# Layer 0's weight folds as two fp32r products, with butterflies on GpSimd and input signs at the exit

## The chip, the cores and the metric

The kernel runs on one core of a Trainium2 chip. The metric is device time in microseconds (us) of one execution of the whole program; several runs are taken and their median is compared. The engines of the core are TensorE (PE in the profile; PEld are its weight loads), VectorE (DVE), ScalarE (ACT), GpSimd (POOL) and SyncE (SP), which here only issues transfers (DMAs). Each engine works through its own queue in order and waits there for what other engines deliver.

## The reference, cut to what matters

Two layers over x of shape 4 x 512 x 512. Each layer is a layer norm, a sequence block `s`, a feed-forward block whose silu is the gate `g`, and `x + s * g`. Layer 0's sequence block is softmax attention with 32 query and 8 key heads of 16. Its feed-forward block is the one that the change touches:

```python
x = fwht(x * SU_ug) / SCALE
x_up = x @ W_up.T * (Wscale_ug[:INTER] * SCALE)
x_gate = x @ W_gate.T * (Wscale_ug[INTER:] * SCALE)
x = silu(x_gate) * x_up
x = fwht(x * SU_dp) / SCALE
x = x @ W_down.T * (Wscale_dp * SCALE)
```

`fwht` is a Walsh-Hadamard transform over the last dimension (512, then 2048), with entries of +1 and -1 before its scale. `SU_ug` and `SU_dp` are vectors of signs. Layer 1 (a gated delta rule and a feed-forward block with signed weights) is not touched.

## The kernel before, in words

**Folding.** The transform is not applied to the activations but to the weights, once, in the first of the four batches: `W` becomes sign x Hadamard x `W`. A Hadamard matrix of 512 is a Kronecker product, so it is applied in two parts: butterflies (sums and differences) over the 4 chunks of 128 rows, and one product with a 128 x 128 Hadamard matrix over the rows of a chunk.

For gate and up weights there are 16 pairs `n` = 0 to 15, each 256 columns of one of the two matrices: a tile `raw` of 128 x 4 x 256 fp32. `load_raw(n)` (L166) loads it, `mix(n, 0)` and `mix(n, 1)` (L240) do the two butterfly levels, from `raw` to `tmp` and back, each level one sum and one difference of 128 x 512 elements (`butterfly`, L48, whose two operations are L52 and L53), on VectorE. `fold(n, j)` (L247), j = 0 and 1, multiplies two chunks by `hs`, the Hadamard matrix with the input signs in it, in fp32, into PSUM. From there ACT writes the product rounded to fp32r (a reduced fp32 that TensorE takes in one pass) as `hi` (L256), and VectorE the rest, `lo` = product - `hi` (L257). Both halves stand in the tile `fo`, which the gate/up products of batch 0 read and which a transfer stores (`wS`, L262) for the later batches. A plain fp32 product takes two passes on TensorE, so each shows as two matmul records.

For the down weights, `mix_down(q)` (L268), q = 0 to 15, multiplies a 128 x 512 piece by a 16-point Hadamard matrix `h16` held in 128 x 128, and writes it to DRAM in another order; `wdn` is loaded back from there (L275), and `fold_down(a)` (L279), a = 0 to 15, multiplies by `hmat` and scales (L282).

**Order.** The work runs in units `u` = 0 to 256. Unit `u` has one step of the attention of a batch (`maxima`: two score products L418 and a VectorE maximum over 1024 elements, L419; `exps`, 11 units later: two products L439 and an exponential on ACT, L441), and, from u = `LATE` = 16 on, one unit of feed-forward work: `v = u - 16`; in v = 0 to 31 of a batch one gate or up product of 8 matmuls (`gate_up`, L326, with its exits L332, L333, L336 on ACT and VectorE and the product L337 on GpSimd), in v = 32 to 63 the `down` products (L344). In batch 0 the folding is put in the units by the table `early`: `mix_down(q)` at u = q; pair `n`, with u = 12 + 2n as its base, has `mix(n, 0)` at base - 3, `mix(n, 1)` at base - 2, `fold(n, 0)` at base and `fold(n, 1)` at base + 1. `fold_down(a)` follows in v = 16 to 31. The library's scheduler may move an operation forward of this order when it holds it ready and the engine free; `keep_in_program_order` (here `inorder`) forbids that for single operations.

**Buffers.** `raw` has 3 buffers, `tmp` one, `fo` 3. The load of pair n + 3 is issued in `fold(n, 1)`. All pool `a0`, where these tiles lie, is given back at v = 32.

**GpSimd** has in this stage only L337 and, once in eight units, the attention's scaling L465. [...]

Of the kernel before, what the change touches and what calls it, by code (L numbers as in the profile page):

```python
# [18 lines left out]
P = 128  # L19
# [3 lines left out]
KC = DM // P  # L23
# [10 lines left out]
def kernel(ctx: ExitStack, tc: tile.TileContext, i: dict, out: bass.AP):  # L34
# [66 lines left out]
    if True:  # L101
# [64 lines left out]
        def load_raw(n):  # L166
            q, m = n // 2, n % 2
            raws[n] = new(a0, [P, KC, CQ], F32, "raw", bufs=3)
            nc.sync.dma_start(
                raws[n], i[("w_gateT", "w_upT")[m]][:, ts(q, CQ)].rearrange("(k p) n -> p k n", p=P)  # L170
            )
# [13 lines left out]
        for q in range(NI):  # L185
            if q in (0, 6, 12):
                load_raw(q // 6)
            nc.sync.dma_start(stage[q], i["w_downT"].rearrange("(p q) n -> q p n", q=NI)[q])
# [20 lines left out]
        for h in (8, 16, 32, 64, 1, 2, 4):  # L209
            nxt = new(a0 if h == 64 else awp, [P, P], F32, "h16" if h == 64 else "hmat", bufs=1 if h == 64 else 2)  # L210
            butterfly(nc.vector, nxt.unsqueeze(2), hmat.unsqueeze(2), P, h, inorder)
            hmat = nxt
            if h == 64:
                h16 = nxt
# [25 lines left out]
        def mix(n, stage):  # L240
            if stage == 0:
                tmps[n] = new(a0, [P, KC, CQ], F32, "tmp")
                butterfly(nc.vector, tmps[n], raws[n], KC, 1)
            else:
                butterfly(nc.vector, raws[n], tmps[n], KC, 2)

        def fold(n, j):  # L247
            q, m = n // 2, n % 2
            if j == 0:
                fos[n] = new(a0, [P, 2, 2, KC, P], F32R, "fo", bufs=3)  # L250
            ph = new(bmm, [P, 2, CQ], F32, "mm")
            for k in range(2):
                nc.tensor.matmul(ph[:, k, :], hs[:, 2 * j + k, :], raws[n][:, 2 * j + k, :], start=True, stop=True)
            ph = ph.rearrange("p k (c n) -> p c k n", n=P)
            hi, lo = fos[n][:, :, 0, 2 * j : 2 * j + 2, :], fos[n][:, :, 1, 2 * j : 2 * j + 2, :]
            nc.scalar.copy(hi, ph)  # L256
            nc.vector.tensor_tensor(lo, ph, hi, ALU.subtract)  # L257
            if j == 0:
                return
            if n + 3 < FF // P:  # L260
                load_raw(n + 3)
            nc.sync.dma_start(  # L262
                wS[ts(q, 2), m].rearrange("c p h k n -> p c (h k n)"),
                fos[n].bitcast(F32).rearrange("p c h k n -> p c (h k n)"),
            )


        def mix_down(q):  # L268
            ph = new(bmm, [P, DM], F32, "mm")
            nc.tensor.matmul(ph, h16, stage[q], start=True, stop=True)  # L270
# [8 lines left out]
        def fold_down(a):  # L279
            ph = misc()  # L280
            nc.tensor.matmul(ph, hmat, wdn[:, a, :], start=True, stop=True)
# [231 lines left out]
        ph = new(bmm, [P, KC, P], F32, "mm")  # L513
        for k in range(KC):
            hk = new(a0, [P, P], F32, "hk", bufs=1)
            inorder(nc.vector.tensor_scalar(hk, hmat, su_ug[:, k : k + 1], None, ALU.mult))
            nc.tensor.transpose(ph[:, k, :], hk, identf)
        hs = new(a0, [P, KC, P], F32, "hs")
        nc.scalar.copy(hs, ph)

# [3 lines left out]
        for n in range(FF // P):  # L524
            u = LATE + 2 * n - 4
            for d, f in ((-3, lambda n=n: mix(n, 0)), (-2, lambda n=n: mix(n, 1)),
                         (0, lambda n=n: fold(n, 0)), (1, lambda n=n: fold(n, 1))):
# [4 lines left out]
        for u in range(NU + LAG + 1):  # L532
# [22 lines left out]
            if 16 <= v < 16 + NI:  # L555
                fold_down(v - 16)
# [901 lines left out]
```

## Time and profile before

| | |
|---|---|
| median of 3 runs | 1493.79 us |
| lowest and highest run | 1490.02, 1494.76 us |
| span of the profiled execution | 1492.3 us |
| instructions in it | 22700 |
| TensorE, VectorE, ACT, GpSimd busy, whole span | 1429.4, 1035.8, 709.6, 313.5 us |
| first fold product L253, last one | 33.1, 164.7 us |
| `mix_down` products L270 | 19.1 to 41.5 us |
| gate/up products of batch 0 (L326 on `fo`) | 43.1 to 180.1 us |
| last butterfly half ends | 152.2 us |
| first `down` product L344 | 183.7 us |

The profile shows one execution. Its lines name an instruction by line of the kernel, engine, operation, tile written and tiles read. Groups give the count, the busy time in us and the mean of one in ns, then how long the engine stood idle before them and what ended that. A timeline line gives start, duration (us), engine, line, operation, and, in brackets, the idle time before it. Matmuls are pipelined: the duration of one record is longer than its distance to the next.

### The profile page before, as it was taken

The page shows a single profiled execution, that of the slowest core. Times are in us where ns is not written, and L with a number is a line of the kernel's source. Part 1 is how long each engine was busy: PE and PEld are TensorE (multiplying, and loading weights), DVE is VectorE, ACT ScalarE, POOL GpSimd, SP SyncE. Part 2 cuts the span into 40 slices and gives each one's busy share as a digit, 9 for nine tenths or more (in the row PEclk, how much of TensorE's full clock was granted, in tenths as well). Part 3 has the DMA queues.
Part 4 walks back from the last instruction along what each step waited for, and adds up shares of the span by engine and source line. Part 5 has one row for each costly group of instructions (what it writes and reads, how often), then busy time and mean ns, then how long its engine had stood idle before and what let it go on. Part 6 is the DMA issues. An engine that isn't in the chain of part 4 may idle for free. (4 is left out here: it accounts for less than half of the span.)

```text
span 1492.3 us, 22700 instructions
## 1 busy us (share of the span) xinstructions
PE 1429.4 (96%) x8144; PEld 855.6 (57%) x8144; DVE 1035.8 (69%) x1863; ACT 709.6 (48%) x1046; POOL 313.5 (21%) x304
## 2 busy tenths in 40 slices
PE   7999999999999999999999899999999999999998
PEld 3565533555335553356434576787568766776675
DVE  7999755765557655666525869768975799477746
ACT  4655554666446664466552434434353344323433
POOL 1112100322003220033100330045112531052001
PEclk9999999999999999999999999999999999999989
DMA  8865410475105741166103553434453354425532
GB/s 307 322 220 194 149 29 16 149 237 190 27 21 190 231 149 28 36 212 225 56 20 103 160 146 101 116 92 147 134 151 103 91 161 135 126 73 150 162 83 96
DMA packets 201793, 199.11 MB, mean 133 GB/s; under 512 B 65520, under 2 KB 153040, under 8 KB 200784
## 3 DMA queue, kind: packets, MB, share of 16 engines
q1 hardware_dynamic: 198624, 196.29, 41.9%
q10 hardware_dynamic: 3056, 1.37, 0.4%
q8 instruction: 64, 1.05, 0.3%
q14 instruction: 49, 0.40, 0.1%
HBM read 146.80 MB, written 46.19 MB: 129 GB/s over the span
## 5 line engine op out<-in xcount | busy, mean ns | idle before, releaser
L419 DVE TENSOR_REDUCE nmx<-sc 128x2 f32<-128x1024 f32 x256 | 312.3, 1220 | 159.1 <-PE st L439 147.3
L441 ACT ACTIVATE pe<-st 128x1024 f16<-128x1024 f32 x256 | 262.6, 1026 | 143.4 <-PE st L439 141.6
L344 PE MATMUL y<-wdn,hT 128*128 128x512 f32 x512 | 253.3, 617 | 3.0 <-DVE g L348 1.7
L326 PE MATMUL mm<-xr,wc 128*128 128x512 f32 x768 | 206.8, 410 | 0.0
L326 PEld LDWEIGHTS mm<-xr,wc 128*128 128x128 f32 x768 | 137.4, 189 | 48.4 <-issue 21.8
L337 POOL TENSOR_TENSOR hT<-hT,th 128x512 f32<-128x512 f32 x64 | 84.2, 1316 | 319.2 <-ACT hT L336 309.0
L344 PEld LDWEIGHTS y<-wdn,hT 128*128 128x128 f32 x512 | 87.0, 189 | 96.0 <-issue 88.5
L711 PE MATMUL pu<-xn1T,wp 128*128 128x512 f32 x288 | 129.9, 594 | 0.0
L941 PE MATMUL ph<-xsh,sg 128*128 128x512 f32 x256 | 113.0, 441 | 5.6 <-ACT sg L926 5.3
L418 PE MATMUL sc<-kT,qT 32*128 32x512 f16 x512 | 102.5, 385 | 7.8 <-DVE nmx L419 7.4
L926 ACT ACTIVATE sg<-sw 128x512 fp32r<-128x512 f32 x128 | 79.5, 625 | 55.2 <-PE y L972 32.2
L941 PE MATMUL ph<-xsl,sg 128*128 128x512 f32 x256 | 104.1, 407 | 0.7 <-DVE xsl L901 0.7
L418 PEld LDWEIGHTS <-qT 32*128 32x128 f16 x512 | 26.2, 91 | 131.8 <-issue 127.9
L465 POOL TENSOR_TENSOR oT<-os,sm 128x512 f16<-128x512 f32 x32 | 41.5, 1298 | 285.9 <-DMA sm<-rec_d 248.8
L439 PE MATMUL st<-qm,kT 32*128 32x512 f16 x512 | 100.0, 384 | 0.3 <-ACT pe L441 0.3
L946 ACT ACTIVATE hT<-ph,upsc 128x512 f32<-128x512 f32 x64 | 43.8, 685 | 94.3 <-PE ph L941 94.1
L711 PEld LDWEIGHTS pu<-xn1T,wp 128*128 128x128 f32 x288 | 54.0, 191 | 56.6 <-issue 54.8
L972 PE MATMUL y<-sg,hsh 128*128 128x512 f32 x256 | 83.0, 432 | 0.7 <-ACT sg L926 0.7
L1019 POOL TENSOR_TENSOR gm<-g,le 128x384 fp32r<-128x384 f32 x64 | 57.8, 921 | 83.0 <-PE pu L1020 52.0
L326 PE MATMUL mm<-xr,fo 128*128 128x512 f32 x256 | 73.2, 420 | 0.9 <-DVE fo L257 0.9
L972 PE MATMUL y<-sg,hsl 128*128 128x512 f32 x256 | 73.5, 400 | 0.0
L332 ACT ACTIVATE th<-mm,hwg 128x512 f32<-128x512 f32 x64 | 44.0, 688 | 56.0 <-PE mm L326 56.0
(302 smaller groups left out, 2370.2 us busy)
## 6 DMA issues: line engine op xcount, KB each, us to landing
wc<-wS SPq DMA_DIRECT2D x96, 512.0 KB
wS<-fo SPq DMA_DIRECT2D x16, 1024.0 KB
sw<-in_upT SPq DMA_DIRECT2D x64, 256.0 KB
sw<-in_downT SPq DMA_DIRECT2D x64, 256.0 KB
sm<-rec_d SPq DMA_DIRECT2D x128, 64.0 KB
raw<-in_w_gateT SPq DMA_DIRECT2D x8, 512.0 KB
hT<-in_w_downT SPq DMA_DIRECT2D x16, 256.0 KB
raw<-in_w_upT SPq DMA_DIRECT2D x8, 512.0 KB
```

The source lines that it names most:

```text
L326: nc.tensor.matmul(pgs[m], wcs[b, c, m][:, h, k, :], xrs[b][:, k, :], start=(k + h == 0), stop=(k == KC - 1 and h == 1))
L337: nc.gpsimd.tensor_tensor(hT, hT, ths[b, c], ALU.mult)
L344: nc.tensor.matmul(ys[t], hTs[b, c][:, ts(t, P)], wdn[:, c, :], start=(c == 0), stop=(c == NI - 1))
L418: nc.tensor.matmul(sc[:, j, :], qTs[n][rows, ts(t, P)], kTs[b, g // 4][rows, :], start=True, stop=True)
L419: nc.vector.tensor_reduce(nmxs[n][:, t, 2 * pr : 2 * pr + 2], sc, AX.X, ALU.max, negate=True)
L439: nc.tensor.matmul(st[:, j, :], kTs[b, g // 4][rows, ts(k, P)], qms[n][rows, :], start=True, stop=True)
L441: nc.scalar.activation(pes[u], st, AF.Exp)
L711: nc.tensor.matmul(pp, wps[b, n][:, k, 0:P], xn1Ts[b][:, k, :], start=(k == 0), stop=(k == KC - 1))
L926: tc.keep_in_program_order(nc.scalar.activation(sgs[b, c, m], raws[b, c, m], AF.Sign))
L941: ins = nc.tensor.matmul(ph, sgs[b, c, 0][:, ts(k, P)], xss[b][n][:, k, :], start=(k + n == 0), stop=(k == KC - 1 and n == 1))
L972: ins = nc.tensor.matmul(yss[b][t], hss[b, c][n][:, ts(t, P)], sgs[b, c, 1], start=(c + n == 0), stop=(c == NI - 1 and n == 1))
L1019: nc.gpsimd.tensor_tensor(gm, bc_in(s["g2"][:, t, u, x], P), bc_mid(le, 3), ALU.mult)
```

## The change

The products with the Hadamard matrix, whose entries are +1 and -1 and exact in fp32r, become two fp32r products: the other operand is split in a rounded half `hi` and a rest `lo`, by a new helper:

```diff
+        def halves_of(src, eng):
+            rh = new(a0, [P, 2, DM], F32R, "rh", bufs=2)
+            hi = rh[:, 0]
+            nc.scalar.copy(hi, src)
+            eng.tensor_tensor(rh[:, 1], src, hi, ALU.subtract)
+            return rh
+
+        rhs = {}
+
+        def part_raw(n, j):
+            rhs[n, j] = halves_of(raws[n][:, 2 * j : 2 * j + 2, :].rearrange("p k n -> p (k n)"), nc.vector)
+            if j == 1 and n + 2 < FF // P:
+                load_raw(n + 2)
```

The signs can't stand in the matrix any more when it is to be the same for all chunks; they are applied when the product leaves PSUM, chunk by chunk:

```diff
             for k in range(2):
-                nc.tensor.matmul(ph[:, k, :], hs[:, 2 * j + k, :], raws[n][:, 2 * j + k, :], start=True, stop=True)
-            ph = ph.rearrange("p k (c n) -> p c k n", n=P)
-            hi, lo = fos[n][:, :, 0, 2 * j : 2 * j + 2, :], fos[n][:, :, 1, 2 * j : 2 * j + 2, :]
-            nc.scalar.copy(hi, ph)
-            nc.vector.tensor_tensor(lo, ph, hi, ALU.subtract)
+                for h in range(2):
+                    nc.tensor.matmul(ph[:, k, :], hmr, rhs[n, j][:, h, ts(k, CQ)], start=(h == 0), stop=(h == 1))
+            for k in range(2):
+                kk = 2 * j + k
+                src = ph[:, k, :].rearrange("p (c n) -> p c n", n=P)
+                hi = fos[n][:, :, 0, kk, :]
+                nc.scalar.activation(hi, src, AF.Copy, scale=su_ug[:, kk : kk + 1])
+                nc.vector.scalar_tensor_tensor(
+                    fos[n][:, :, 1, kk, :], src, su_ug[:, kk : kk + 1], hi, ALU.mult, ALU.subtract
+                )
             if j == 0:
                 return
-            if n + 3 < FF // P:
-                load_raw(n + 3)
```

The butterflies go to GpSimd, the down products are split too (with the rest on GpSimd), and the loads, the matrices and the order follow:

```diff
-            raws[n] = new(a0, [P, KC, CQ], F32, "raw", bufs=3)
+            raws[n] = new(a0, [P, KC, CQ], F32, "raw", bufs=2)
...
-            if q in (0, 6, 12):
-                load_raw(q // 6)
+            if q in (0, 8):
+                load_raw(q // 8)
...
             if h == 64:
-                h16 = nxt
+                h16r = new(a0, [P, P], F32R, "h16r")
+                inorder(nc.vector.tensor_copy(h16r, nxt))
+        hmr = new(a0, [P, P], F32R, "hmr")
+        inorder(nc.vector.tensor_copy(hmr, hmat))
...
-                butterfly(nc.vector, tmps[n], raws[n], KC, 1)
+                butterfly(nc.gpsimd, tmps[n], raws[n], KC, 1)
             else:
-                butterfly(nc.vector, raws[n], tmps[n], KC, 2)
+                butterfly(nc.gpsimd, raws[n], tmps[n], KC, 2)
...
         def mix_down(q):
+            rh = halves_of(stage[q], nc.gpsimd)
             ph = new(bmm, [P, DM], F32, "mm")
-            nc.tensor.matmul(ph, h16, stage[q], start=True, stop=True)
+            for h in range(2):
+                nc.tensor.matmul(ph, h16r, rh[:, h], start=(h == 0), stop=(h == 1))
...
         def fold_down(a):
+            rh = halves_of(wdn[:, a, :], nc.gpsimd)
             ph = misc()
-            nc.tensor.matmul(ph, hmat, wdn[:, a, :], start=True, stop=True)
+            for h in range(2):
+                nc.tensor.matmul(ph, hmr, rh[:, h], start=(h == 0), stop=(h == 1))
...
-        ph = new(bmm, [P, KC, P], F32, "mm")
-        for k in range(KC):
-            hk = new(a0, [P, P], F32, "hk", bufs=1)
-            inorder(nc.vector.tensor_scalar(hk, hmat, su_ug[:, k : k + 1], None, ALU.mult))
-            nc.tensor.transpose(ph[:, k, :], hk, identf)
-        hs = new(a0, [P, KC, P], F32, "hs")
-        nc.scalar.copy(hs, ph)
...
             for d, f in ((-3, lambda n=n: mix(n, 0)), (-2, lambda n=n: mix(n, 1)),
+                         (-1, lambda n=n: part_raw(n, 0)), (0, lambda n=n: part_raw(n, 1)),
                          (0, lambda n=n: fold(n, 0)), (1, lambda n=n: fold(n, 1))):
...
-            if 16 <= v < 16 + NI:
-                fold_down(v - 16)
+            for a in range(NI):
+                if v == 8 + 3 * a // 2:
+                    fold_down(a)
```

So a pair's raw halves are split at base - 1 and base, `fold_down` stands in v = 8 to 30 instead of 16 to 31, and the tile `rh` with its two buffers is shared by the raw halves, `mix_down` and `fold_down`.

More of the change, by code (lines that the diff above doesn't have):

```diff
@@ L209 @@
         for h in (8, 16, 32, 64, 1, 2, 4):
[L210 removed]
+            nxt = new(a0, [P, P], F32, "hmat", bufs=2)
             butterfly(nc.vector, nxt.unsqueeze(2), hmat.unsqueeze(2), P, h, inorder)
```

## The prediction

> **What bounds the kernel now.** I read the slices first, then the stage in which the edited lines run, then its rows. The chain of waits covers only the kernel's last 110 us, so it says nothing of this stage.
>
> ```profile
> span 1492.3 us, 22700 instructions
> ...
> PE   7999999999999999999999899999999999999998
> ...
> DVE  7999755765557655666525869768975799477746
> ...
> POOL 1112100322003220033100330045112531052001
> ```
>
> A slice is 37.3 us. Over the whole span TensorE (PE) is the full row. VectorE (DVE) is full only in slices 2 to 4, and GpSimd (POOL) is nearly empty there. Those slices are layer 0's first batch, where the weights are folded. By stage (us; busy time of PE, weight loads, DVE, ACT, POOL; clock, DMA share, GB/s):
>
> ```profile
> 15.00:183.00 168.00, 159.94 (x759) 92.48 (x757) 153.95 (x224) 93.33 (x133) 27.59 (x20) 1.00 0.64 233
> ...
> 115.00:150.00 35.00, 32.00 (x150) 19.34 (x148) 34.97 (x48) 17.64 (x24) 8.71 (x6) 1.00 0.53 191
> 150.00:183.00 33.00, 32.37 (x160) 19.29 (x160) 25.60 (x42) 18.58 (x25) 6.38 (x5) 1.00 0.33 121
> ```
>
> From 115 to 150 us DVE is busy 34.97 of 35.00: it sets the pace, with PE close behind. After 150 us, when the butterflies are over, PE does. How far PE is from its own limit is seen in a later batch, whose gate/up units have no folds:
>
> ```profile
> 690.06 2.13 PE L326 MATMUL mm<-xr,wc 128*128 128x512 f32 x8
> ...
> 692.44 2.13 PE L326 MATMUL mm<-xr,wc 128*128 128x512 f32 x8
> ```
>
> 2.38 us a unit there. The first batch's 32 units run from 43.1 to 180.1 us, 4.28 us each. Everything after 183 us is untouched by the edit, so the change is worth what it moves the end of this stage.
>
> **DVE, part by part.** The rows of this stage (count | busy us, mean ns | idle before):
>
> ```profile
> L257 DVE TENSOR_TENSOR fo<-mm,fo 128x512 fp32r<-128x512 f32 x32 | 21.8, 681 | 2.9 <-ACT fo L256 2.9
> L53 DVE TENSOR_TENSOR tmp<-raw 128x512 f32<-128x512 f32 x16 | 14.1, 881 | 0.0
> L53 DVE TENSOR_TENSOR raw<-tmp 128x512 f32<-128x512 f32 x16 | 12.9, 808 | 0.0
> L52 DVE TENSOR_TENSOR raw<-tmp 128x512 f32<-128x512 f32 x16 | 11.9, 743 | 0.1
> ...
> L52 DVE TENSOR_TENSOR tmp<-raw 128x512 f32<-128x512 f32 x16 | 11.6, 728 | 2.5 <-DMA raw<-in_w_upT 1.3 <-DMA hT<-in_w_downT 1.1
> ```
>
> Off DVE go 64 butterfly halves (14.1+12.9+11.9+11.6 = 50.5 us), four `hk` scalings (4 x 0.28 = 1.1) and 32 old residues (21.8). On it come 32 residues of the raw weights (0.68 each by the butterflies' median: 21.8), and 64 residues of 256 elements from PSUM: 0.678 us at 512 elements (L333) and 0.352 at 192 (L1201) are 1.02 ns an element, so 0.42 each, 26.9. Two casts of the Hadamard matrix add 0.4. Net: -50.5 - 1.1 - 21.8 + 21.8 + 26.9 + 0.4 = **-24.3 us** before waiting.
>
> Waiting is the open price, because the new residues read two SBUF operands while GpSimd reads SBUF:
>
> ```profile
> 115.10 1.55 POOL L465 TENSOR_TENSOR oT<-os,sm 128x512 f16<-128x512 f32 x1 [1.28 <-DMA sm<-rec_d]
> ...
> 115.43 1.76 DVE L53 TENSOR_TENSOR raw<-tmp 128x512 f32<-128x512 f32 x1
> ...
> 144.54 1.28 POOL L465 TENSOR_TENSOR oT<-os,sm 128x512 f16<-128x512 f32 x1 [4.91 <-DMA wS<-fo]
> 144.56 0.67 DVE L257 TENSOR_TENSOR fo<-mm,fo 128x512 fp32r<-128x512 f32 x1
> ```
>
> The first pair reads SBUF on both sides: DVE took 1.76 us for what takes 0.68. In the second DVE reads one operand from PSUM, and nothing is lost. The butterflies lost on average (50.5 - 64 x 0.68)/64 = 0.11 us with POOL busy 27.6 of 168 us; the worst lost 1.1. With POOL nearly always busy, half of its 1.28 us is the middle: I take 0.6, bounds 0.11 and 1.1, so 32 x 0.6 = 19 us (3.5 to 35). DVE's net is then -5 us (-21 to +11).
>
> [...]
>
> **POOL.** On it come 64 butterfly halves, 16 residues in `mix_down` and 16 in `fold_down`; 16 products L337 and 4 of L465 are there already. Price of one, back to back:
>
> ```profile
> 641.19 1.29 POOL L337 TENSOR_TENSOR hT<-hT,th 128x512 f32<-128x512 f32 x1 [1.57 <-ACT hT L336]
> 642.44 1.17 POOL L485 TENSOR_TENSOR x<-sg,xin 128x512 f32<-128x512 f32 x1
> ```
>
> 1.25 us. Program order puts ahead of the last butterfly (unit 40) the 16 `mix_down` residues, 64 halves, 12 L337, 3 L465 and 11 `fold_down` residues: 106 x 1.25 = 132.5 us, from 15.4 us, when the first raw weights are there. [...] That is 15.4 + 132.5 + 19 = 167 us; the last butterfly ends at 152.2 today.
>
> **The raw buffers**, 3 to 2, and the load behind the raw residue instead of behind the fold. A load lands late:
>
> ```profile
> 102.97 0.37 SPq L169 DMA_DIRECT2D raw<-in_w_upT  x1
> ...
> 108.37 0.69 DVE L52 TENSOR_TENSOR tmp<-raw 128x512 f32<-128x512 f32 x1 [0.37 <-DMA raw<-in_w_upT]
> ```
>
> 5.4 us from issue to use. After a pair's second butterfly come two ACT copies and two DVE residues, behind a maximum of 1.22 us in DVE's queue (about 3.5 us), then 5.4 for the load: 8.9. POOL meanwhile has 4 halves (5.0), one L337 (1.25), 0.3 of L465, 1.2 of port and from unit 24 on 1.67 of `fold_down`: 7.8, later 9.4. So it idles about 1 us in the early pairs and little later; SP's queue adds to it, since L169 stands there behind stores that wait up to 5.8 us (L262). I take 0.7 us in 12 pairs: 8.5 us (0 to 18). Queued behind POOL's waiting butterfly are L337 and the `fold_down` residues; PE's folds wait for both.
>
> **The end by POOL.** 167 + 8.5 = 175.5. Then the last pair's copy, residue and fold, 0.62 + 1.28 + 0.78 + 0.37 + 0.42 = 3.5, and 1.0 of hand-overs: 180. Then the three units that need it or stand behind it, at 2.38 + 0.53 for a `fold_down`: 8.7, and 1.5 to the first `down`: **190.2 against 183.7**, +6.5.
>
> **PE.** `mix_down` and `fold_down`: six passes of L270 take 2.84 us, so (2.84 - 0.59)/5 = 0.45 a pass, two passes a product; fp32r of that shape takes 2.13/8 = 0.266. 32 x 2 x 0.18 = 11.5 us less. The folds keep their count: four fp32 passes of 256 take 0.78 (130.21 to 130.99); four fp32r lie between four weight loads, 0.75, and 4 x 0.266 = 1.06. I take 0.78, the same load count (-1 to +9 us in all). PE waits for POOL here, so this gain is in slack, as are the four transposes removed. **ACT** gains the 64 copies of high halves, 32 of raw weights and 32 for the two down steps (0.62 each, as L926 from SBUF: 39.7), and 64 scaled copies of 256 elements (0.37 each, between L256's 0.587 at 512 and L441's 1.025 at 1024, by the same slope: 23.7) in place of 32 of 0.587 (18.8); the `hs` copy, 0.6, goes. 93.3 + 44 = 137 of 168 us. Covered, unless it waits for `rh`, below. DMA bytes are unchanged; the second raw load goes out two `w_downT` loads later, covered by POOL's first 14 operations; moving `fold_down` to units 24 to 46 needs `wdn` earlier (84 instead of 115 us), and its loads go out at 51 today; some 15 us later still does.
>
> **Sum.** 1492.3 + 6.5, and the 1.5 us by which the median of the runs (1493.79) stands above the profiled span: **1500 us**.
>
> **The rivals.** *The relief wins.* For it: DVE is full and loses 24 us before waits; POOL's sum without port and idle loss is 15.4 + 132.5 = 148, earlier than today's 152.2. Then PE paces: 43.1 + 32 x 2.38 + 28 folds x 0.78 + 16 x 0.53 + 7 for values and queries = 156.7, 27 us earlier. Against: no engine stays idle long enough for all of that; half is -13: 1481. *The split buffers jam ACT*, the case on the slow side beyond mine: `rh` has two buffers for three users, one held by the raw half that waits for its fold. ACT's copy for `fold_down` or a raw half stands in order ahead of the exponentials; if it waits until POOL has passed one or two butterflies (1.25 to 2.5 us), 16 `fold_down` and 16 `mix_down` steps cost 32 x 1.9 = 61 us, of which ACT's slack 168 - 137 = 31 covers half. It decides once that wait exceeds 1 us a step: about +25 with part of the above, 1519. *Nothing moves*: DVE's 5 us net and POOL's 6 offset each other, 1494.
>
> **Chances.** POOL as bound, 1497 to 1510: 0.40. Relief: 0.29. Jam: 0.17. Nothing: 0.14. A measurement of this kernel tells 0.3% (4.5 us) from no change. Of my case 0.03 falls within it; of the nothing case 0.12, the rest on the sides: faster 0.30, same 0.15, slower 0.55. The range, 1479 to 1522, takes the relief down to its middle and the jam up to its own.
>
> **What would show it.** POOL busy over 85% from 20 to 165 us; residues of the raw weights above 1.1 us mean; the last butterfly after 165 us; the first `down` matmul near 190. The last butterfly before 150, or residues near 0.75, would show the relief; ACT copies waiting long for a PE release, the jam. I am wrong if POOL is not the last to deliver to the folds.

## The result, and the profile after

The changed kernel takes 1557.38 us (median of 4 runs, 1555.01 to 1558.02) against 1493.53 us: a ratio of 1.0431, 95% interval 1.0414 to 1.0448. The profiled execution has a span of 1555.5 us, 63.2 more than before. The forecast, 1500 us, had the direction, but the loss was ten times the size, and the range (to 1522) did not hold it.

The slices of the kernel after, to be read against those of before (a slice is now 38.9 us):

```profile
span 1555.5 us, 22937 instructions
...
PE   4787889999999999999999989999999999999998
...
DVE  5676775567655765566651687957994789567746
...
POOL 5457872022300322013310042025310541143001
PEclk9588879999999999999999999999999999999989
```

The first six slices, up to about 233 us, look different: before, PE was full from the second slice on and VectorE in three of them; now nothing is. PE stands at 4 to 8, VectorE at 5 to 7, and GpSimd, which my forecast had as the bound, at 4 to 8 as well. The granted clock, 1.00 in the stage before, is 0.5 in one of them. The windows of the kernel after show it by stage (busy time of PE, weight loads, VectorE, ACT, GpSimd; clock, DMA share, GB/s):

```profile
15.00:33.00 18.00, 11.55 (x61) 5.70 (x61) 9.49 (x19) 7.60 (x14) 10.99 (x9) 0.97 0.62 206
33.00:80.00 47.00, 34.62 (x94) 14.33 (x94) 26.90 (x36) 27.92 (x48) 23.68 (x19) 0.50 0.36 132
80.00:115.00 35.00, 28.57 (x142) 18.09 (x140) 28.07 (x45) 24.18 (x39) 18.74 (x15) 0.81 0.72 264
115.00:150.00 35.00, 25.82 (x116) 17.20 (x115) 19.66 (x29) 17.97 (x33) 25.61 (x20) 0.87 0.50 177
150.00:183.00 33.00, 28.28 (x109) 17.64 (x108) 24.45 (x34) 20.01 (x35) 26.31 (x20) 0.83 0.33 116
```

When every engine has gaps, the likely bound is a chain of hand-overs and not work. The waits of the kernel after between 15 and 240 us name its links (engine, tile and line that waited, who released it: us in total, times, longest):

```profile
POOL rh L254 <- ACT rh L253: 29.1, 14, 5.8
...
POOL hT L361 <- ACT hT L360: 23.2, 9, 5.0
ACT hT L293 <- PE mm L292: 22.7, 15, 4.6
DVE nmx L443 <- PE sc L442: 21.4, 13, 4.9
...
PEld mm L292 <- POOL rh L254: 13.7, 13, 4.6
ACT rh L253 <- POOL raw L52: 11.6, 8, 3.2
PEld y L305 <- POOL rh L254: 11.1, 8, 2.8
```

It is a ring: GpSimd's rest (L254) waits for ACT's high half (L253), PE's product (L292, L305) for GpSimd's rest, ACT's exit (L293) for PE's product, and ACT's next high half stands behind that exit. The timeline of the kernel after shows one turn in the `mix_down` stage (start, duration, engine, line; in brackets the idle time before):

```profile
34.56 1.14 ACT L253 CAST rh<-hT 128x512 fp32r<-128x512 f32 x2
...
35.24 2.14 PE L292 MATMUL mm<-rh,h16r 128*128 128x512 f32 x3 [0.65 <-ACT rh L253]
35.26 2.50 POOL L254 TENSOR_TENSOR rh<-hT,rh 128x512 fp32r<-128x512 f32 x2 [2.06 <-ACT rh L253]
...
37.41 0.59 ACT L293 COPY hT<-mm 128x512 f32<-128x512 f32 x1 [1.71 <-PE mm L292]
...
37.81 0.79 PE L292 MATMUL mm<-rh,h16r 128*128 128x512 f32 x1 [0.43 <-POOL rh L254]
...
38.64 0.59 ACT L293 COPY hT<-mm 128x512 f32<-128x512 f32 x1 [0.64 <-PE mm L292]
39.12 1.14 ACT L253 CAST rh<-hT 128x512 fp32r<-128x512 f32 x2
39.19 1.23 DVE L443 TENSOR_REDUCE nmx<-sc 128x2 f32<-128x1024 f32 x1 [3.33 <-PE sc L442]
```

Two steps take 4.56 us (34.56 to 39.12; the next turn begins at 43.70): 0.70 us to the first copy's hand-over, 1.25 for each of two rests, 0.79 for the last pass, an exit. The exit waits for the same last pass that sets a buffer of `rh` free, so this turn alone does not say whether the next copy waits for its place behind the exit or for the buffer. The maximum of the attention (L443) waits too, because its scores stand behind L292 in PE's order. In the timeline of the kernel before, the same product needed nothing but its loaded operand, and six passes, three steps, ran in 2.84 us:

```profile
26.91 2.84 PE L270 MATMUL mm<-hT,h 128*128 128x512 f32 x6
```

With the attention's work between them, the 16 steps took 22.4 us before and take 54.6 after.

In time: the first fold product comes at 54.6 us (33.1 before), the last at 231.4 (164.7), the first `down` at 246.0 (183.7). So of the 62.3 us by which this stage ends later, 21.5 are a later start of the folds, 45.2 a slower pace over the 16 pairs (176.8 us from first to last against 131.6), and 4.4 are regained behind the last fold. The rest of the kernel is as long as it was (1309.5 against 1308.6 us).

### The profile page after: what moved, and what is told of

Its sections match the earlier page's. It is cut to its first block, busy times and chain, and to the rows that moved or that the text cites. A ratio compares the mean times of both kernels' runs of the same rounds, so it can differ in the third digit from the quotient of the medians.

```text
span 1555.5 us, 22937 instructions
## 1 busy us (share of the span) xinstructions
PE 1447.3 (93%) x8140; PEld 865.8 (56%) x8140; DVE 1038.0 (67%) x1861; ACT 752.1 (48%) x1142; POOL 439.2 (28%) x400
## 5 line engine op out<-in xcount | busy, mean ns | idle before, releaser
L443 DVE TENSOR_REDUCE nmx<-sc 128x2 f32<-128x1024 f32 x256 | 312.4, 1220 | 183.0 <-PE st L463 149.8
L350 PEld LDWEIGHTS mm<-xr,wc 128*128 128x128 f32 x768 | 136.7, 188 | 48.2 <-issue 21.5
L442 PE MATMUL sc<-kT,qT 32*128 32x512 f16 x512 | 108.6, 400 | 12.5 <-DVE nmx L443 12.2
L463 PE MATMUL st<-qm,kT 32*128 32x512 f16 x512 | 106.2, 395 | 2.1 <-ACT pe L465 2.0
L944 ACT ACTIVATE sg<-sw 128x512 fp32r<-128x512 f32 x128 | 79.6, 625 | 57.2 <-PE y L990 33.1
L729 PEld LDWEIGHTS pu<-xn1T,wp 128*128 128x128 f32 x288 | 53.9, 191 | 56.6 <-issue 55.1
L350 PE MATMUL mm<-xr,fo 128*128 128x512 f32 x256 | 78.5, 449 | 2.2 <-ACT hT L360 1.4
```

The lines of the kernel that those rows point to most:

```text
L350: nc.tensor.matmul(pgs[m], wcs[b, c, m][:, h, k, :], xrs[b][:, k, :], start=(k + h == 0), stop=(k == KC - 1 and h == 1))
L442: nc.tensor.matmul(sc[:, j, :], qTs[n][rows, ts(t, P)], kTs[b, g // 4][rows, :], start=True, stop=True)
L443: nc.vector.tensor_reduce(nmxs[n][:, t, 2 * pr : 2 * pr + 2], sc, AX.X, ALU.max, negate=True)
L463: nc.tensor.matmul(st[:, j, :], kTs[b, g // 4][rows, ts(k, P)], qms[n][rows, :], start=True, stop=True)
L729: nc.tensor.matmul(pp, wps[b, n][:, k, 0:P], xn1Ts[b][:, k, :], start=(k == 0), stop=(k == KC - 1))
L944: tc.keep_in_program_order(nc.scalar.activation(sgs[b, c, m], raws[b, c, m], AF.Sign))
```

## The experiments

"Over before" is the ratio less one, times 1493.5 us. The three times on the right are those of the profiled execution: first and last fold product, first `down` product.

| kernel | ratio, 95% interval | over before, us | folds, us | `down`, us |
|---|---|---|---|---|
| before | 1 | 0 | 33.1 to 164.7 | 183.7 |
| after | 1.0431, 1.0414 to 1.0448 | 64 | 54.6 to 231.4 | 246.0 |
| e1_butterflies_only | 1.0043, 1.0025 to 1.0060 | 6 | 35.1 to 167.6 | 186.3 |
| e2_split_only | 1.0354, 1.0336 to 1.0372 | 53 | 43.5 to 223.8 | 239.0 |
| e3_mix_down_fp32 | 1.0271, 1.0249 to 1.0293 | 40 | 40.3 to 205.7 | 220.3 |
| e4_downs_fp32 | 1.0153, 1.0132 to 1.0174 | 23 | 38.1 to 190.2 | 206.1 |
| e9_downs_fp32_three_raw | 1.0078, 1.0051 to 1.0104 | 12 | 37.8 to 176.9 | 192.8 |
| e13_butterflies_signs | 1.0034, 1.0014 to 1.0055 | 5 | 34.4 to 169.0 | 187.6 |
| e5_three_rh | 1.0377, 1.0346 to 1.0408 | 56 | 48.6 to 218.3 | 232.9 |
| e6_own_rh | 1.0433, 1.0398 to 1.0468 | 65 | 69.5 to 229.7 | 244.8 |
| e7_kept_warm | 1.0427, 1.0399 to 1.0454 | 64 | 52.1 to 228.2 | 242.7 |
| e8_rest_on_dve | 1.0325, 1.0294 to 1.0355 | 49 | 46.8 to 207.6 | 223.5 |
| e16_after_the_norm | 1.0428, 1.0394 to 1.0462 | 64 | 52.4 to 231.8 | 246.4 |
| e19_half_ahead | 1.0358, 1.0324 to 1.0392 | 53 | 47.1 to 216.8 | 231.2 |
| e15_no_product_on_gpsimd | 1.0388, 1.0357 to 1.0418 | 58 | 53.9 to 225.2 | 240.5 |
| e18_mix_down_split | 1.0073, 1.0052 to 1.0093 | 11 | 43.2 to 177.2 | 196.0 |
| e12_fold_down_split | 0.9988, 0.9971 to 1.0006 | -2 | 35.1 to 164.9 | 182.3 |
| e17_fold_down_split_butterflies | 0.9979, 0.9960 to 0.9999 | -3 | 36.3 to 164.1 | 181.0 |
| e14_butterflies_no_product | 0.9988, 0.9965 to 1.0010 | -2 | 34.8 to 161.2 | 180.2 |
| e10_first_level | 1.0076, 1.0049 to 1.0102 | 11 | 35.2 to 171.5 | 190.3 |

What follows the first `down` took between 1307.0 and 1319.6 us in these profiles, so a few us at the end of the stage need not show in the time.

### One half of the change each

**Butterflies alone**, the kernel before with

```diff
-                butterfly(nc.vector, tmps[n], raws[n], KC, 1)
+                butterfly(nc.gpsimd, tmps[n], raws[n], KC, 1)
...
-                butterfly(nc.vector, raws[n], tmps[n], KC, 2)
+                butterfly(nc.gpsimd, raws[n], tmps[n], KC, 2)
```

> The kernel before, with one edit: the 64 butterfly halves go to GpSimd. No split, three raw buffers, fp32 products. If the split and its two shared buffers are what costs (theory A), VectorE loses 50 us of work, keeps no instruction with two SBUF operands of that size, and the stage ends earlier by 10 to 20 us: 1475 to 1485. If butterflies on GpSimd are the harm, by the port or by standing behind the products of L337 in GpSimd's queue (theory B), the gate/up units slow down as in the changed kernel, and it takes 1515 or more.

Measured: +6 us (1503.33), between the two theories' ranges, so neither held. **The split alone**, the kernel after with these four lines the other way round:

> The changed kernel with the butterflies back on VectorE; splits, signs at the exit, order and buffers stay. Theory A: the first gate/up product still comes near 80 us, and the whole stays above 1535. Theory B: the first gate/up product comes before 55 us and the whole falls to 1510 or less.

Measured: +53 us (1549.72), theory A's time, though the first gate/up product came at 67.9 us and not near 80. The two add up to 59 of the 64. Most of the loss belongs to the split and what comes with it (two raw buffers, signs, order), not to 64 slower butterflies on a busier engine.

### Taking the split apart

The kernel after with the product of `mix_down`, and then of `fold_down` too, left as one plain fp32 product:

```diff
-            rh = halves_of(stage[q], nc.gpsimd)
...
-            for h in range(2):
-                nc.tensor.matmul(ph, h16r, rh[:, h], start=(h == 0), stop=(h == 1))
+            nc.tensor.matmul(ph, h16, stage[q], start=True, stop=True)
```

> The changed kernel with mix_down in one fp32 product again; raw halves and fold_down stay split, butterflies stay on GpSimd. Theory A with mix_down as the main user of the two rh buffers in the first 80 us: the first gate/up product comes near 45 us instead of 81, the clock stays at full there, and the whole falls by 30 to 40 us to 1518 to 1528. If the late start comes from GpSimd (butterflies) instead, it stays within 10 us of 1557.

> As the one before, and fold_down in one fp32 product too, so that the two rh buffers serve the raw halves alone. Theory A, with fold_down as a jam of the gate/up units: those 32 units take 140 us or less instead of 163, and the whole 1495 to 1505. If the units are slow for another reason (GpSimd's queue, the smaller exits), it stays within 5 us of the one before.

Measured: +40 and +23 us; so 24 us are given back with `mix_down`'s split and 18 more with `fold_down`'s. Both have theory A's direction and less than its size: gate/up starts at 55.0 us instead of near 45 in the first, and the second takes 1520.65 us instead of 1495 to 1505. Two thirds of the loss lie in the two steps that I had down as saving 11.5 us of PE. In `fold_down` the chain of the kernel after looks like this:

```profile
123.74 0.61 ACT L253 CAST rh<-wdn 128x512 fp32r<-128x512 f32 x1
...
124.43 1.28 POOL L52 TENSOR_TENSOR tmp<-raw 128x512 f32<-128x512 f32 x1
...
125.36 0.39 PE L305 MATMUL y<-rh,hmr 128*128 128x512 f32 x1
...
125.68 1.26 POOL L53 TENSOR_TENSOR tmp<-raw 128x512 f32<-128x512 f32 x1
126.90 1.26 POOL L254 TENSOR_TENSOR rh<-wdn,rh 128x512 fp32r<-128x512 f32 x1
128.21 0.19 PEld L305 LDWEIGHTS y<-rh,hmr 128*128 128x128 f32 x1 [2.66 <-POOL rh L254]
128.21 0.50 PE L305 MATMUL y<-rh,hmr 128*128 128x512 f32 x1 [2.35 <-POOL rh L254]
```

The high half is copied at 123.74 and its pass runs at 125.36. The rest stands behind two butterflies on GpSimd and starts only at 126.90, 1.15 us after that pass has ended; PE stands 2.35 us, and the gate/up products behind it start at 129.31. Over all 16 steps the waits put PE's matmuls down to these rests for 7.8 us. In e2, where no butterflies stand in GpSimd's queue, it is still 4.0 us.

With both down steps back to fp32, **the third raw buffer** and the load three pairs ahead:

```diff
-            raws[n] = new(a0, [P, KC, CQ], F32, "raw", bufs=2)
+            raws[n] = new(a0, [P, KC, CQ], F32, "raw", bufs=3)
...
-            if q in (0, 8):
-                load_raw(q // 8)
+            if q in (0, 6, 12):
+                load_raw(q // 6)
...
-            if j == 1 and n + 2 < FF // P:
-                load_raw(n + 2)
+            if j == 1 and n + 3 < FF // P:
+                load_raw(n + 3)
```

> The kernel after with both down products left as plain fp32 (as e4_downs_fp32, 1520.65 us), and the raw weights with three buffers and the loads three pairs ahead, as before the change. Theory A (what is left of the loss in e4_downs_fp32 is GpSimd waiting for raw loads, 28.8 us in six waits there, because there are two buffers): 1504 to 1510, first down product at 189 to 195. Rival B (it is the chain of the split itself, copy, residue, product, exit, in an order that PE and ACT cannot leave): 1515 to 1521, first down product above 200.

Measured: +12 us (1508.94), in theory A's range for the time and for the first `down` (192.8). So the two buffers cost 11 us here. How is shown only in part: GpSimd's waits for raw loads fall from 28.8 to 21.1 us, and in the kernel after itself, where all is later, they are 4.9 us.

And with the raw halves gone too, only **butterflies and signs at the exit** are left, the folds being plain fp32 products with `hmat`:

> The kernel before with the butterflies on GpSimd and the signs applied at the exit (two copies and two residues of 256 elements in place of one of 512 each), the folds still one plain fp32 product. Theory (the 64 smaller exits cost ACT 64 x 0.477 - 18.8 = 12 us and VectorE 64 x 0.478 - 21.8 = 9 us, which e1_butterflies_only leaves room for): 1503 to 1507, within 4 us of e1_butterflies_only. Rival (the exits, two hand-overs longer with only three product buffers, are the cost left in e4_downs_fp32): 1510 to 1518.

Measured: +5 us (1501.17, two below the theory's range and within the 4 us of e1 that it allowed): the 64 smaller exits cost nothing that shows. From e9 to here 7 us go: the raw split proper (its copies and residues, the casts of the matrices at the start), together with the earlier place of `fold_down` and the later raw loads, which also go back.

In this order of removal the 64 us are: `mix_down` split 24, `fold_down` split 18, raw buffers 11, raw split with order 7, butterflies and signs 5 (rounded; unrounded they add up to 64).

### Is it the shared buffers, the clock, or the engine of the rest?

Three buffers `rh` instead of two; the down steps with one buffer of their own beside the two of the raw halves; four more fp32r products in each `mix_down` step, whose result is overwritten, to keep PE busy; and the rests of the down steps on VectorE:

```diff
-            rh = new(a0, [P, 2, DM], F32R, "rh", bufs=2)
+            rh = new(a0, [P, 2, DM], F32R, "rh", bufs=3)
```

> The changed kernel with three rh buffers instead of two, shared as before. If the shortage of rh buffers is what holds the start (theory A1), the 16 mix_down steps, 54.6 us from 24.6 to 79.2 in the changed kernel, shrink to 40 us or less and the whole falls by 15 us or more. If the serial hand-over on the engines' own queues (copy on ACT, rest on GpSimd, product, exit on ACT) and the halved clock hold it (theory A2), the gain is under 10 us.

```diff
-            rh = halves_of(stage[q], nc.gpsimd)
+            rh = halves_of(stage[q], nc.gpsimd, "rd", 1)
...
-            rh = halves_of(wdn[:, a, :], nc.gpsimd)
+            rh = halves_of(wdn[:, a, :], nc.gpsimd, "rd", 1)
```

> The changed kernel with rh's two buffers for the raw halves alone and one buffer of its own for mix_down and fold_down. Theory A1 in the form that the raw halves wait behind mix_down for a buffer: the first fold product, at 54.6 us in the changed kernel, comes before 42 us, and the first gate/up product before 65. With one buffer mix_down itself gets no faster. Theory A2: first fold product later than 48 us, and the whole within 10 us of the changed kernel.

```diff
             ph = new(bmm, [P, DM], F32, "mm")
+            for _ in range(4):
+                nc.tensor.matmul(ph, h16r, xrs[0][:, 0, :], start=True, stop=True)
```

> The changed kernel with four more fp32r products of 512 columns in each mix_down, into the same bank ahead of the real ones, which overwrite them: 16 x 4 x 0.27 = 17 us more work for TensorE, all of it where it waits today. If the halved clock is a cause of its own (theory C), the granted clock between 33 and 80 us goes from 0.5 to near 1 and the whole falls by 5 to 15 us in spite of the work. If the clock only follows from the waiting, the whole stays within 5 us or rises by up to 15.

```diff
-            rh = halves_of(stage[q], nc.gpsimd)
+            rh = halves_of(stage[q], nc.vector)
...
-            rh = halves_of(wdn[:, a, :], nc.gpsimd)
+            rh = halves_of(wdn[:, a, :], nc.vector)
```

> The changed kernel with the rests of mix_down and fold_down taken by VectorE instead of GpSimd. If GpSimd's queue and its 1.27 us a rest set the pace of the mix_down stage (theory D), a rest takes 0.7 us and does not stand behind butterflies: the stage shrinks from 54.6 to 35 us or less and the whole falls by 20 us or more. If buffers and ACT set it, it falls by less than 10.

Measured: 56, 65, 64 and 49 us over before. A third buffer gives back 8, as theory A2 had it (under 10). The rest on VectorE, at the median 0.69 us in both steps instead of 1.27 and 1.28 on GpSimd, gives back 15, between the two expectations (the stage takes 45.4 us, not 35); its first `down` comes 22.5 us earlier. One buffer of their own makes `mix_down` a strict sequence (24.4 to 88.1 us, 4.2 us a step; the first fold at 69.5 us is theory A2's) while the folds, with two buffers for themselves, pass faster (160.2 us); the two cancel. The clock did rise when PE had more to do (busy 41.60 of 47.00 us against 34.62), as the window of e7 shows over the stretch that the second window of the kernel after covers:

```profile
33.00:80.00 47.00, 41.60 (x155) 23.19 (x154) 31.34 (x47) 30.52 (x52) 23.34 (x19) 0.78 0.39 137
```

0.78 against 0.50, and the time is the same, in spite of the added products. Where the clock was nearly back (0.89 from 34 to 47 us, against 0.50) the passes were shorter: over the stage a pass of `mix_down` took 0.40 us at the median, against 0.79. But the stage ends at 77.5 instead of 79.2 us and the first `down` comes 3.3 us earlier, which the time does not show. So I read the half clock as mostly what the waiting leaves behind; that it costs nothing is not shown, since e7 adds work as it raises the clock. In the kernel after the clock falls within a pause of PE of 4.14 us that ends at 33.25 us (1.00 up to 31.5 us, 0.50 from 32.0 us). Between 34 and 47 us it stays at 0.50, with PE busy 10.10 of 13.00 us and listed pauses of 0.43 to 0.65 us.

### The order of the steps and of the start

The two halves of `mix_down` step q + 1 ahead of the product of step q (with three `rh`), and the first two high copies of `mix_down` pinned behind the layer norm:

```diff
         def mix_down(q):
-            rh = halves_of(stage[q], nc.gpsimd)
+            if q == 0:
+                part_down(0)
+            if q + 1 < NI:
+                part_down(q + 1)
+            rh = rhs["down", q]
```

> e5_three_rh (the kernel after with three buffers rh, 1549.43 us) with the two halves of mix_down step q + 1 issued ahead of the product of step q. Theory A (the stage is slow because each step's copy, rest, product and exit follow one another in program order, so that one unit ahead hides the rest): mix_down ends at 50 to 60 us instead of 72.5, 1530 to 1540. Rival B (three users on three buffers, and GpSimd's butterflies ahead of the rest, hold it all the same): 68 us or later, 1546 to 1556.

Measured: 53 us over before, against 56 in e5_three_rh: theory A nearly had the stage, rival B has the time. `mix_down` ends at 60.9 instead of 72.5 us and gate/up begins at 64.1 instead of 73.3, but the last fold comes at 216.8 instead of 218.3. Of these 9 us 1.7 come through at the first `down`. That ends the reading, which I held until then, that the `mix_down` stage costs time because gate/up starts behind it. What counts, as I read it now, is when the folds of the 16 pairs come, and their copies, rests and exits stand in the same three queues.

```diff
-            nc.scalar.copy(hi, src)
+            pin(nc.scalar.copy(hi, src))
...
-            rh = halves_of(stage[q], nc.gpsimd)
+            rh = halves_of(stage[q], nc.gpsimd, inorder if q < 2 else lambda ins: ins)
```

> The kernel after with the high copies of mix_down 0 and 1 kept in program order, behind the first layer norm, instead of moved ahead of it. Theory A (ACT waits 8.57 us for w_downT ahead of the norm's square root, so all starts 4 to 5 us late): transposes at 10.6 instead of 15.08, and the time 4 us less, 1552 to 1555. Rival (the start is covered, since the mix_down stage paces what follows and ends as late): 1556 to 1559.

The start of the kernel after has two oddities in its timeline:

```profile
3.15 3.65 DVE L215 CAST h16r<-hmat 128x128 fp32r<-128x128 f32 x1
...
4.88 1.84 POOL L325 MEMSET vp<- 128x1024 f16 x2
...
7.64 0.23 DVE L217 CAST hmr<-hmat 128x128 fp32r<-128x128 f32 x1
...
11.59 1.25 ACT L253 CAST rh<-hT 128x512 fp32r<-128x512 f32 x2 [8.57 <-DMA hT<-in_w_downT]
...
14.16 0.21 ACT L68 ACTIVATE lnrs<-lnrs 128x4 f32<-128x4 f32 x1
```

The cast of a 128 x 128 matrix takes 3.65 us while GpSimd clears memory and 0.23 afterwards; and ACT waits 8.57 us for a piece of `w_downT`, moved ahead of the norm's square root, on which everything else waits. Measured with the copies pinned: the first transposes come at 12.3 instead of 15.1 us, and the time is 64 us over before, as without. The start is covered, as the rival said (1562.27 us, 3 above its range, at the ratio of the kernel after).

### The two down splits by themselves

In the kernel before, one split each, with two buffers that nothing else uses, the rest on GpSimd:

```diff
         def fold_down(a):
+            rh = new(a0, [P, 2, DM], F32R, "rh", bufs=2)
+            hi = rh[:, 0]
+            nc.scalar.copy(hi, wdn[:, a, :])
+            nc.gpsimd.tensor_tensor(rh[:, 1], wdn[:, a, :], hi, ALU.subtract)
             ph = misc()
-            nc.tensor.matmul(ph, hmat, wdn[:, a, :], start=True, stop=True)
+            for h in range(2):
+                nc.tensor.matmul(ph, hmr, rh[:, h], start=(h == 0), stop=(h == 1))
```

> The kernel before with fold_down alone as two fp32r products (high half on ACT, rest on GpSimd, two buffers that nothing else uses); butterflies stay on VectorE. Theory A (the split costs where its buffers and GpSimd's queue are shared with the raw halves and butterflies; alone it is hidden, and PE saves 16 x 0.36 = 5.8 us where it is the bound): 1488 to 1492. Rival B (the hand-over ACT, GpSimd, PE stands in PE's order in any case, 2 us a step for half of the 16 steps): 1503 to 1512.

> The kernel before with mix_down alone as two fp32r products (high half on ACT, rest on GpSimd, two buffers that nothing else uses); butterflies on VectorE, GpSimd otherwise nearly free. Theory A (the step itself is a chain of copy, rest, product and exit that ACT and PE run in program order, two steps per 4.57 us at the best seen): mix_down ends at 60 to 70 us, gate/up starts there, 1508 to 1518. Rival B (the chain was slow only because raw halves and butterflies share its buffers and GpSimd): mix_down ends at 41 to 48 us, 1490 to 1498.

The second is the same edit in `mix_down`, with `h16r` and `stage[q]`. A third is `fold_down`'s split together with the butterflies of e1. In all three the four `hk` tiles of the start stand in the buffer of `tmp`, to make room.

> e12_fold_down_split (fold_down alone as two fp32r products, own buffers; 1495.16 us) with the butterflies on GpSimd as well. Theory A (GpSimd's queue is what makes fold_down's rest late: it stands behind butterflies, which wait for raw loads): 1512 to 1520, GpSimd's rest released late for PE. Rival B (it was the sharing of the two buffers with the raw halves; with its own buffers the split stays free): 1500 to 1505, as e1_butterflies_only (1503.33).

Measured: -2 us for `fold_down` (1495.16, three above theory A's range and far below rival B's), +11 for `mix_down`, -3 for the third. In these two kernels `fold_down`'s split is free, even with GpSimd fuller than it ever is in the kernel after. The window of e17 over 120 to 160 us:

```profile
120.00:160.00 40.00, 37.30 (x188) 24.93 (x187) 28.01 (x37) 24.78 (x38) 38.91 (x32) 1.00 0.47 159
```

GpSimd is busy 38.91 of 40.00 us, the clock is 1.00, and the kernel is no slower than before: a full GpSimd alone does not make this split dear. Its timeline shows why:

```profile
126.16 1.28 POOL L285 TENSOR_TENSOR rh<-wdn,rh 128x512 fp32r<-128x512 f32 x1
...
131.32 0.62 PE L288 MATMUL y<-rh,hmr 128*128 128x512 f32 x2
```

The rest is there 3.9 us before its product, and both passes run in 0.62 us. The halves are issued right in front of the product here too, but the products lie 3.7 us or more apart, behind the gate/up products, and with two buffers of its own a pair of halves is made a step ahead. Over all 16 steps PE's matmuls wait 0.7 us for rests, and not at all in e12, against 7.8 in the kernel after. Rival B held, with a time 6 us below its range; theory A did not.

`mix_down`'s split alone does cost, with two buffers of its own as well. The chain of its timeline, in e18:

```profile
36.72 0.62 ACT L272 CAST rh<-hT 128x512 fp32r<-128x512 f32 x1
37.13 0.55 PEld L276 LDWEIGHTS mm<-rh,h16r 128*128 128x128 f32 x2 [0.48 <-POOL rh L273]
...
37.42 1.35 POOL L273 TENSOR_TENSOR rh<-hT,rh 128x512 fp32r<-128x512 f32 x1 [0.34 <-ACT rh L272]
37.97 0.59 ACT L277 COPY hT<-mm 128x512 f32<-128x512 f32 x1 [0.63 <-PE mm L276]
38.45 0.62 ACT L272 CAST rh<-hT 128x512 fp32r<-128x512 f32 x1
```

One step takes 1.73 us (36.72 to 38.45): GpSimd's rest of 1.35 us and 0.34 to 0.39 us in which it waits for ACT's next copy, which stands behind an exit. The stage ends at 54.1 instead of 41.5 us, the folds start 10.2 us later and then keep the pace of before (134.0 us against 131.6). That is 11 us of its 24 in the kernel after, between theory A's place (60 us or later) and rival B's, with a time just inside theory A's.

### Why the butterflies cost anything

Only the first level on GpSimd; and all of them there, but the products of gate and up (L337) of the first batch on VectorE; and the same product off GpSimd in the kernel after:

```diff
-                nc.gpsimd.tensor_tensor(hT, hT, ths[b, c], ALU.mult)
+                (nc.vector if b == 0 else nc.gpsimd).tensor_tensor(hT, hT, ths[b, c], ALU.mult)
```

> The kernel before with the first butterfly level on GpSimd, the second still on VectorE; nothing else changed. Theory (VectorE at 34.97 of 35.00 us sets the pace of the middle of the stage and is relieved by 32 halves, 26 us, while GpSimd has 40 us and stays far ahead): first down product 4 to 10 us earlier, 1484 to 1490. Rival (e1_butterflies_only lost 6 us with all of them moved, since the port and the waits on loads give back what VectorE gains): 1494 to 1500.

> e1_butterflies_only (butterflies on GpSimd, 1503.33 us) with the 16 products of gate and up of the first batch on VectorE instead of GpSimd. Theory (GpSimd waits 41 us in e1_butterflies_only for a high copy on ACT ahead of that product, and the next pair's butterflies stand behind it; VectorE has room for 16 x 0.68 = 11 us): those waits go, first down product at 176 to 183, 1488 to 1496. Rival (the butterflies are late because of the raw loads and their doubled price, 1.25 against 0.79 us; the wait for the product was only their slack): 1500 to 1505.

> The kernel after with the 16 products of gate and up of the first batch on VectorE instead of GpSimd. Theory A (GpSimd waits 23.2 us for ACT ahead of that product with the next pair's butterflies behind it, about half of which comes through to the folds): 1542 to 1550. Rival B (the folds wait for ACT's copies and for rh, so GpSimd's waits only move to another place): 1554 to 1559.

Measured: +11, -2 and +58 us. Half the butterflies cost no less than all of them (1510.06 us, worse than both expectations; the two intervals just overlap), so it is not their number. In the waits of e10 one line leads, and it leads in e1_butterflies_only with 41.1 us:

```profile
POOL hT L337 <- ACT hT L336: 60.0, 13, 9.5
...
POOL tmp L52 <- DMA raw<-in_w_upT: 23.2, 4, 15.5
ACT hT L336 <- PE mm L326: 21.0, 15, 2.4
```

GpSimd stands 60 us with a product whose operand ACT has not delivered, and the butterflies of the next pair stand behind it. In e10's timeline the longest such wait is followed by butterflies that wait for nothing else:

```profile
68.51 1.27 POOL L337 TENSOR_TENSOR hT<-hT,th 128x512 f32<-128x512 f32 x1 [9.51 <-ACT hT L336]
69.74 1.28 POOL L52 TENSOR_TENSOR tmp<-raw 128x512 f32<-128x512 f32 x1
```

At other places a raw load is late too, 23.2 us in four waits. In the kernel before the same product waits 141.1 us, with no butterflies behind it. With the product taken off GpSimd's queue, the 6 us of e1 are gone (1496.02 us, the upper end of the theory's range; the first `down` comes at 180.2, 6.0 us earlier than in e1). In the kernel after the same edit gives back about 6 us too, at the near edge of its rival's range; the two intervals still overlap a little. The rival's mechanism is there as well: GpSimd's waits for high copies grow from 29.1 to 41.9 us.

## Why the prediction was wrong

**What held.** The change is worth what it moves the end of this stage: 62.3 us at the first `down`, 63.2 in the span. The work on each engine was counted nearly right. Over the whole span VectorE went from 1035.8 to 1038.0 us (+2.2, forecast -5), ACT from 709.6 to 752.1 (+42.5, forecast +44), GpSimd from 313.5 to 439.2 (+125.7, forecast 139). The single prices, from the groups of the kernel after (count | busy us, mean ns | idle before):

```profile
L254 DVE TENSOR_TENSOR rh<-raw,rh 128x512 fp32r<-128x512 f32 x32 | 31.6, 993 | 4.6 <-ACT rh L253 4.4
...
L277 DVE SCALAR_TENSOR_TENSOR fo<-mm,su_ug,fo 128x256 fp32r<-128x256 f32 x64 | 30.3, 478 | 18.9 <-ACT fo L276 18.9
L276 ACT ACTIVATE fo<-mm,su_ug 128x256 fp32r<-128x256 f32 x64 | 29.9, 477 | 21.0 <-PE mm L350 10.1 <-PE mm L271 6.7 <-DVE fo L277 4.0
```

A raw residue took 0.31 us more than my 0.68 (0.99), half of the 0.6 that I had added and within its bounds. No run shows a port, or the term that the sum has under that name on GpSimd (19 us, and 1.2 a pair): the 96 halves and rests there took 128.4 us in the kernel after, 1.34 each, against 1.28 a half in e1, 5.5 us more in all. The exits of 256 elements take 0.48 us on both engines where I had 0.42 and 0.37. The fold passes came out at 0.74 for four against 0.78. The raw buffers cost 11 us, in the order of removal above, against 8.5 (0 to 18). One reading was off and had no part in the sum: VectorE's row shows nines in four later slices too, outside this stage.

**What failed.** Three steps, and they are one mistake.

First, *PE waits for POOL here, so this gain is in slack*, together with the sum that began at 15.4 us on GpSimd and left the first 43 us of the kernel as they were. (GpSimd's first butterfly came at 21.8 us, and gate/up at 81.2.) I priced the two down products by their passes on PE (0.45 to 0.266 us a pass) and never wrote down the chain that a step had become: high copy 0.62, rest 1.26, last pass and exit, through two buffers, ACT's copy standing behind the exit. For `mix_down` that is 2.28 us a step in the kernel after and 1.73 in e18, where nothing else is split, while before three steps in a row took 2.84. The gain in passes was not in slack, it was gone: the two splits cost 42 us (24 and 18 by e3 and e4), where the sum held nothing for them but GpSimd's work and set 11.5 us down as slack.

Second, ACT's *Covered, unless it waits for `rh`*. The sum of 137 of 168 us said nothing of order. The rival that I built from that doubt, *the split buffers jam ACT*, named the right steps, `mix_down` and `fold_down`, and priced the waiting raw at 61 us; then it took half off as covered by ACT's slack and kept 25. The slack of one engine covered nothing here, where three engines waited for each other in turn, each in its own order. Its mechanism was right in part only: its sign, copies on ACT waiting for a release of `rh` by PE, is small (the largest such wait in the kernel after is 6.7 us in total), a third buffer gave back 8 us, and the waits stand elsewhere in the ring: GpSimd for high copies (29.1), PE for rests (15.4), ACT's exits for PE (22.7). I gave this rival 0.17.

Third, *POOL as the bound*, my likeliest case at 0.40. Its signs failed: GpSimd is busy 50 to 80% of the windows up to 183 us, not 85, since it waits 29.1 us for high copies and 23.2 for the gate copies; the raw residues took 0.99 us, not over 1.1; the first `down` came at 246.0 us, not near 190. Its last butterfly does end late (218.4 us; forecast 175.5 with the raw loads, before 152.2), but late from waiting. And e17, with GpSimd 97% busy for 40 us, is no slower than before: a full GpSimd would not have been the bound.

The case in which the relief of VectorE wins (0.29) fell as well, also without the split: with the butterflies on GpSimd and no loss left from it (e14, e17) the time is that of before, within 0.3%. VectorE was full from 43 to 150 us, but PE was at 32.00 of 35.00 beside it, and 26 to 50 us of butterflies taken off VectorE (e10, e14, e17) brought the first `down` forward by 3.4 us at most.

**What stays open.** How `fold_down`'s 18 us divide between the two buffers that it shares with the raw halves and its earlier place (units 24 to 46) isn't shown: e12 and e17 differ from the kernel after in both, and they do not split the raw weights. The butterflies ahead of the rests have a part in it too (7.8 us of waits of PE's matmuls with them, 4.0 without, in e2). `mix_down` loses 11 us alone and 24 in company; e5 and e8 move a part of the other 13, e6 and e19 hardly any. Here as well rests stand behind butterflies: at 33.25 us PE had waited 4.14 us for one. Why e17 is 10 us faster than e1, when its products save PE only 16 x 0.4 us, is not settled; GpSimd's wait for the gate copies falls from 41.1 to 11.2 us there. e14 and e17 together were not tried; neither alone beats the kernel before by more than its measurement tells.

## What to carry to other kernels

A product that is split in two needs a copy (here 0.62 us), a rest (1.26) and a hand-over before it can run; count that chain through its buffers and in each engine's program order, at the place where the step stands, before counting the passes that it saves. Where other work lay between the steps, as for `fold_down` in e12 and e17, two buffers of its own let the halves run a step ahead, and the split was free (-2 and -3 us). Where the steps followed each other closely, as for `mix_down` in e18, the chain itself set the pace, 1.73 us a step, in spite of two buffers of its own. And what goes onto an idle engine's queue must not come to stand behind an instruction that waits for another engine (60.0 us in e10).

## What the runs showed of the hardware

**The clock.** In the kernel after it was 0.50 from 33 to 80 us, in which PE was 74% busy by its records; the listed pauses were 0.43 to 0.65 us between 34 and 47 us and none was above 1.81 us after that. In e18 it was 0.50 between 34 and 44 us with PE busy 8.62 of 10.00. By the length of the passes it had fallen there at about 30.5 us (two passes of L276 took 0.73 us at 26.05, 1.02 at 30.31 and 1.22 at 31.99), without a long pause: from 27 to 30.5 us PE was busy 1.95 of 3.50, and no listed pause was above 0.84 us.

**VectorE beside GpSimd.** In e18 the butterflies are on VectorE and the rests on GpSimd. From 34 to 43 us the three halves that started 0.13 to 0.15 us after a rest had begun took 1.76 us each, and the three that started when a rest had 0.07 or 0.08 us left took 0.67 or 0.68:

```profile
35.27 0.67 DVE L52 TENSOR_TENSOR raw<-tmp 128x512 f32<-128x512 f32 x1
...
35.74 1.34 POOL L273 TENSOR_TENSOR rh<-hT,rh 128x512 fp32r<-128x512 f32 x1 [0.39 <-ACT rh L272]
35.87 1.76 DVE L53 TENSOR_TENSOR raw<-tmp 128x512 f32<-128x512 f32 x1
```

A VectorE cast from and to SBUF took 3.65 us beside GpSimd's clearing of memory (from 3.15 to 6.80 us; the clears end at 6.72) and 0.23 without it; two small VectorE operations of 0.17 us (the scales of 128 x 16) took 1.25 and 1.20 beside GpSimd's butterflies. My estimate of 0.6 us a residue, with GpSimd nearly always busy, was not reached on average: it was 0.31 with GpSimd 50 to 80% busy.
